# An AdaLN and routed FFN block in fp32: five of the last block's seven products taken to a second level of Strassen's scheme

## The chip, the cores and the metric

The kernel runs on one core of a Trainium2 chip. The metric is device time in microseconds (us): the median of three runs was 262.04 us (261.8 to 263.51). One execution was recorded by the profiler; it took 261.56 us, of which the profile's span covers 259.8 us. All data are float32.

The engines are named as the profile names them: PE (TensorE, matrix products into the PSUM banks), ACT (ScalarE), DVE (VectorE), POOL (GpSimd) and SP, which here only issues transfers.

## The reference, cut to what matters

There are 64 batches of 64 rows, 512 features wide. Two matrix products of 4096 x 512 x 512 bound the work.

```python
# first part: y = relu(((n*v + sum_n v) * relu(q@W3 + b3)) @ W2 + b2)
q_emb = relu(q @ W3 + b3)
y = relu(((n * v + v_sum) * q_emb[:, None, :]) @ W2 + b2)
# second part, on y
base_out   = y @ W_base + b_base
shared_out = (y @ A_s) @ B_s
gates      = softmax(y @ W_router + b_router)          # 6 experts
topk_w, topk_i = top_k(gates, 2)                       # w_per_e: weight of each expert, 0 if not chosen
hw = einsum('bsd,edr->bser', y, A_r) * w_per_e[..., None]
routed_out = einsum('bser,erf->bsf', hw, B_r)
out = x + base_out + shared_out + routed_out
```

## The kernel before

The tokens are cut into four blocks (`NB`) of 1024. Features lie on the 128 partitions, in four chunks of 128; a block's tokens lie along the free axis in two halves of 512 (`TB`). The main loop runs over the blocks k = 0 to 3. Each block has two products: the *first* makes y from the modulated input and `w2_sb`, the *second* makes the output from y and `wb_sb`. Between them a small product (L779, tile `ph`) computes the 112 low-rank activations (16 shared, 6 x 16 routed) and the 6 router logits of every token.

Both large products use the Strassen-Winograd scheme. Features and tokens are halved, and seven products P1 to P7 of half size stand in place of eight. Sums of the weights (`weight_sums`) and sums of the activations (`row_sums`, tile `sy`) are their operands. P1 and P2 make the quarter C11 of the output; with U = P1 + P6, C12 is U + P5 + P3, C21 is U + P7 + P4 and C22 is U + P7 + P5. A seed is an ACT copy from one PSUM bank to another (`seed`, L629), into which TensorE then accumulates the next product. In the first product of blocks 1 to 3 (`first_inner`) each of the seven is again cut into seven matmuls of 128 x 128 x 256 columns, q1 to q7, with two banks for each of the seven rounds (a and b), seeds on ACT, and sums taken out by DVE and ACT (`take_w5`, `take_u`, `take_22`, `take_1`, `take_21`).

The second product (`second`) has one level: each of P1 to P7 is two output chunks of two matmuls of 512 columns (`product`, L168 to L170), written by hand in the order in which it is to run on TensorE. During it DVE runs the gate (`gate`: softmax, ranks of the experts, weights `w`), then multiplies the activations in `ph` by the weights (tile `hw`, L683). TensorE turns `hw` by eight transposes (tile `pt`, L704), ACT copies them out (`hwT`, L706), POOL makes the difference of the two halves (`hwd`, L708), and TensorE adds the routed part to each of the eight output banks by a matmul of `bcat_sb` with `hwT` or `hwd` (L641). The base bias (`bb_sb`) is added by DVE together with x (`with_x`, L637). DVE adds from the bank to the x rows (`leave`, L662), and SP sends them out. x rows are loaded anew for this by `load_rows` into the buffers of the first product's temporaries.

In blocks 0 to 2, DVE and ACT also prepare the next block in the meantime: a list of steps, `behind`, is drawn upon by `fill` and `share`. In the last block that list is empty. There the last output chunk is split in 384 and 128 columns, the second sent by ACT's queue (L650 to L663).

The order of instructions on each engine is the order in which the program issues them; waits between engines are put in by the framework from what each instruction reads and writes. Tiles of a pool wait until a buffer is free: `ps_p` has six PSUM banks, `ps_h` the place of `ph` and `pt`, `xpool` three places of 16 KB a partition.

Of the kernel before, what the change touches and what calls it, by code (L numbers as in the profile page):

```python
# [9 lines left out]
F32 = mybir.dt.float32  # L10
# [22 lines left out]
HC = GR + E  # L33


@with_exitstack
def adaln_ffn(ctx: ExitStack, tc: tile.TileContext, xa, x0, x1, head, w3, w2, wb, a, bcat, br, outT):
# [47 lines left out]
    NH0 = NQ * B + 3 * NC  # L85
    head_sb = const.tile([P, NH0 + NQ * P], F32, tag="head_sb", name="head_sb")
    cond_sb = head_sb[:, : NQ * B].rearrange("p (c b) -> p c b", c=NQ)
    b3_sb, b2_sb, bb_sb = (head_sb[:, NQ * B + n * NC : NQ * B + (n + 1) * NC] for n in range(3))
# [30 lines left out]
    bcat_sb = loaded(bcat, [GR, D], "bcat_sb")  # L119
    load_x(1)  # L120

# [22 lines left out]
    def inner_weight_sums(w, t, name):  # L144

        at = {i: n for n, i in enumerate((5, 6, 7, 4, 1, 2, 3))}
        it = const.tile([P, 4, 7, P], F32, tag=name, name=name)

        def side(o, n):
            b = {1: t[o][:, 0, :P], 2: t[o][:, 1, :P], 3: t[o][:, 1, P:]}  # L150
            return b[n] if n in b else it[:, {5: 0, 6: 1, 7: 2, 4: 3}[n], at[o]]

        low = w.rearrange("p (o k) m -> p o k m", k=KH)
        groups = ((slice(0, 4), lambda c, m: t["sums"][:, :, c, ts(m, P)]),
                  (slice(4, 6), lambda c, m: low[:, :, c, ts(m, P)]),
                  (slice(6, 7), lambda c, m: t[3][:, c, ts(m, P)].unsqueeze(1)))
        steps = []
        for o, b in groups:
            i = [it[:, n, o] for n in range(4)]
            steps += [  # L160
                lambda i=i, b=b: nc.vector.tensor_tensor(i[0], b(0, 1), b(0, 0), ALU.subtract),
                lambda i=i, b=b: nc.vector.tensor_tensor(i[1], b(1, 1), i[0], ALU.subtract),
                lambda i=i, b=b: nc.vector.tensor_tensor(i[2], b(1, 1), b(0, 1), ALU.subtract),
                lambda i=i, b=b: nc.vector.tensor_tensor(i[3], b(1, 0), i[1], ALU.subtract),
            ]
        return side, steps
# [88 lines left out]
    def row_sums(a, name, cols=slice(0, TB)):  # L255

        all_s = mid.tile([P, 4, KH, TB], F32, tag=name, name=name)
        s = [all_s[:, i, :, cols] for i in range(4)]
        a11, a12, a21, a22 = a[:, :KH, 0, cols], a[:, KH:, 0, cols], a[:, :KH, 1, cols], a[:, KH:, 1, cols]

        def steps(c=slice(0, KH)):
            return [
                lambda: nc.vector.tensor_tensor(s[0][:, c], a21[:, c], a22[:, c], ALU.add),
                lambda: nc.vector.tensor_tensor(s[1][:, c], s[0][:, c], a11[:, c], ALU.subtract),
                lambda: nc.vector.tensor_tensor(s[2][:, c], a11[:, c], a21[:, c], ALU.subtract),
                lambda: nc.vector.tensor_tensor(s[3][:, c], a12[:, c], s[1][:, c], ALU.subtract),
            ]

        return {1: a11, 2: a12, 3: s[3], 4: a22, 5: s[0], 6: s[1], 7: s[2], "sums": all_s}, steps
# [28 lines left out]

    def prepare_inner(k):
# [13 lines left out]
        def steps(g, a, engine=nc.vector):  # L313
            return [
                lambda: engine.tensor_tensor(s[g][:, 0], a(0, 1), a(1, 1), ALU.add),
                lambda: engine.tensor_tensor(s[g][:, 1], s[g][:, 0], a(0, 0), ALU.subtract),
                lambda: engine.tensor_tensor(s[g][:, 2], a(0, 0), a(0, 1), ALU.subtract),
                lambda: engine.tensor_tensor(s[g][:, 3], a(1, 0), s[g][:, 1], ALU.subtract),
            ]

# [253 lines left out]
    def gate(k, ph):  # L574
# [10 lines left out]
        nc.scalar.activation(g, lg, AF.Exp)  # L585
        sm = small.tile([P, 2 * NS], F32, tag="sm", name=f"sm_{k}")
# [11 lines left out]
        nc.vector.tensor_tensor(eq, gj, ge, ALU.is_equal)  # L598
        nc.vector.tensor_tensor(gt, gj, ge, ALU.is_gt)
        nc.vector.tensor_tensor(eq, eq, tri.unsqueeze(1).to_broadcast(pair), ALU.mult)  # L600
        nc.vector.tensor_tensor(gt, gt, eq, ALU.add)
        rank = small.tile(shape, F32, tag="rank", name=f"rank_{k}")
# [13 lines left out]
    def second(k, y, ph, res):  # L616
# [17 lines left out]
        def with_x(name, j, f, h):  # L634

            t = row(f, h)
            nc.vector.scalar_tensor_tensor(t, ps[name, j], bb_sb[:, f : f + 1], t, ALU.add, ALU.add)  # L637
            return t
# [9 lines left out]
        def part(p, cols, i, start):  # L648
            for c in range(KH):
                nc.tensor.matmul(  # L650
                    p[:, cols], tb[i][:, c, ts(1, P)], sy[i][:, c, cols], start=start and c == 0, stop=False,
                    skip_group_check=True,
                )

        def last_routed(p, cols, hw):
            nc.tensor.matmul(
                p[:, cols], bcat_sb[:, ts(KH + 1, P)], hw[:GR, cols], start=False, stop=True,
                skip_group_check=True,
            )

        def leave(p, f, h, add, cols=slice(0, TB), queue=nc.sync):
            nc.vector.tensor_tensor(add[:, cols], p[:, cols], add[:, cols], ALU.add)  # L662
            queue.dma_start(outT[k, f, h, :, cols], add[:, cols])  # L663
# [5 lines left out]
        def share():  # L669
# [12 lines left out]
        hw = small.tile([P, 2 * NS, GR], F32, tag="hw", name=f"hw_{k}")  # L682
        nc.vector.tensor_tensor(  # L683
            hw.rearrange("p s (g r) -> p s g r", r=R),
            ph[:, :, :GR].rearrange("p s (g r) -> p s g r", r=R),
            w.unsqueeze(3).to_broadcast([P, 2 * NS, G, R]),
            ALU.mult,
        )
# [12 lines left out]
        pt = ps_h.tile([P, 2 * NS, P], F32, tag="ph", name=f"pt_{k}")  # L701
        hwT = small.tile([P, 2, TB], F32, tag="hwT", name=f"hwT_{k}")
        for s in range(2 * NS):
            nc.tensor.transpose(pt[:GR, s, :], hw[:, s, :], ident)  # L704
        for h in range(2):
            nc.scalar.copy(hwT[:GR, h], pt[:GR, ts(h, NS)].rearrange("p s t -> p (s t)"))  # L706
        hwd = small.tile([P, TB], F32, tag="hwd", name=f"hwd_{k}")
        nc.gpsimd.tensor_tensor(hwd[:GR], hwT[:GR, 0], hwT[:GR, 1], ALU.subtract)  # L708
# [4 lines left out]
        routed("x", 0, 0, hwT[:GR, 0])  # L713
        finish("x", 0, 0, 0)
        routed("z", 0, 0, hwT[:GR, 1])
        finish("z", 0, 0, 1)

        routed("w", 0, KH, hwT[:GR, 1])
        leave(ps["w", 0], KH, 1, u22[0])
        share()  # L720
        if k < NB - 1:
            prod(5, 1, "w")
            routed("w", 1, KH + 1, hwT[:GR, 1])
            leave(ps["w", 1], KH + 1, 1, u22[1])
        else:
            last = [(ps_p.tile([P, TB], F32, tag="pp", name=f"last_{lo}"), slice(lo, hi), queue)
                    for lo, hi, queue in ((0, 3 * P, nc.sync), (3 * P, TB, nc.scalar))]
            for p, cols, queue in last:
                part(p, cols, 5, True)
                last_routed(p, cols, hwT[:, 1])  # L730
                leave(p, KH + 1, 1, u22[1], cols, queue)
        share()
        routed("x", 1, 1, hwT[:GR, 0])
# [3 lines left out]
        routed("z", 1, 1, hwT[:GR, 1])  # L737
# [3 lines left out]
        routed("w", 0, KH, hwd[:GR])  # L741
        leave(ps["w", 0], KH, 0, u12[0])
        share()
        if k < NB - 1:
            prod(3, 1, "w", start=False)
            routed("w", 1, KH + 1, hwd[:GR])
            leave(ps["w", 1], KH + 1, 0, u12[1])
            return
        for p, cols, queue in last:
            part(p, cols, 3, False)  # L750
            last_routed(p, cols, hwd)
            leave(p, KH + 1, 0, u12[1], cols, queue)
# [4 lines left out]
    inner_t, inner_steps = inner_weight_sums(w2_sb, t2, "inner_t")  # L757
    for k in range(NB):
        y = mid.tile([P, NC, 2, TB], F32, tag="y", name=f"y_{k}")
        rest = None  # L760
        if k == 0:
            first_mixed(y)
        else:
            rest = first_inner(k, y)
        res = load_rows(k)
        if k == 0:
            load_x(3)

        ph = ps_h.tile([P, 2 * NS, P], F32, tag="ph", name=f"ph_{k}")
        groups = [(h, s) for h in range(2) for s in range(NS)]
        if not rest:
            groups.sort(key=lambda g: g[1] // KH)
        for n, (h, s) in enumerate(groups):
            if rest and n == 2:
                rest()
            for c in range(NC):
                nc.tensor.matmul(  # L779
                    ph[:, h * NS + s, :HC], y[:, c, h, ts(s, P)], a_sb[:, c, :],  # L780
                    start=(c == 0), stop=(c == NC - 1),
                )
        sys_[k], steps = row_sums(y, "sy")
        for step in steps():
            step()
        fill(4 if k else 9)
        second(k, y, ph, res)
# [50 lines left out]
```

## Time and profile before

| what | us |
|---|---|
| median of three runs | 262.04 (261.8 to 263.51) |
| the profiled execution | 261.56 |
| its span | 259.8 |
| PE busy | 254.8 (98%) |
| DVE busy | 193.9 (75%) |
| ACT busy | 136.5 (53%) |
| POOL busy | 38.7 (15%) |
| last block: router's groups (L779) end, second product begins | 224.69 |
| last matmul ends | 256.56 |
| last DVE add ends | 256.88 |

The times in the profile's rows are microseconds from the span's start, and the mean durations in its groups are nanoseconds. A matmul of float32 appears as two records. "Idle before" is the time that an engine stood still before an instruction, with what released it.

### The profile page before, as it was taken

What the parts mean: (1) busy time and instruction counts of PE and PEld (TensorE: products, weight loads), DVE (VectorE), ACT (ScalarE), POOL (GpSimd) and SP (SyncE); (2) the same over time, 40 slices, a digit from 0 to 9 for tenths busy, and PEclk for the clock granted to TensorE, in tenths of its full rate; (3) what the DMA queues carried; (4) which work ended last, traced back from release to release, by engine and by line L of the source; (5) the groups of instructions that cost most, each with busy time, mean ns of one, the idle gap of its engine ahead of it and who ended that gap; (6) DMA issues with size and microseconds to landing.
All of it is one profiled execution on the core that took longest, in us unless ns stands there. A gap on an engine that the chain in (4) does not pass through costs nothing.

```text
span 259.8 us, 3177 instructions
## 1 busy us (share of the span) xinstructions
PE 254.8 (98%) x1004; PEld 164.5 (63%) x1004; DVE 193.9 (75%) x386; ACT 136.5 (53%) x373; POOL 38.7 (15%) x53
## 2 busy tenths in 40 slices
PE   7999999999999999999999999999999999999995
PEld 3756896454478888444458889544447889745453
DVE  2899898799968967968995894988895475872332
ACT  2399496596048896289017889349404428112000
POOL 1000000020017610002006630002001770000100
PEclk9999999999999999999999999999999999999999
DMA  6997629303320044000521025200332023400233
GB/s 194 360 352 295 261 99 390 156 3 121 121 81 0 11 156 161 0 3 6 196 81 42 0 83 168 76 0 3 121 121 81 0 77 92 159 0 3 76 139 108
DMA packets 14145, 28.54 MB, mean 110 GB/s; under 512 B 1472, under 2 KB 2496, under 8 KB 14128
## 3 DMA queue, kind: packets, MB, share of 16 engines
q1 hardware_dynamic: 13840, 28.21, 30.6%
q8 instruction: 8, 0.13, 0.2%
q10 hardware_dynamic: 288, 0.13, 0.2%
q14 instruction: 9, 0.07, 0.1%
HBM read 19.94 MB, written 8.39 MB: 109 GB/s over the span
## 4 chain that ended last, share of the span: by engine, by line
PE 94%; ACT 2%; DMA 2%; SPq 0%; issue 0%; DVE 0%
PE ia L446 13%; PE ph L779 11%; PE oz L170 11%; PE ox L170 11%; PE ib L446 10%; PE ow L170 9%; PE py L354 5%; PE oy L170 5%; PE ow L641 5%; PE oz L641 3%; PE ox L641 3%; DMA w_sb<-in_w_dram 2%; PE yw L170 1%; PE pt L704 1%; PE last L650 1%; PE yz L170 1%
## 5 line engine op out<-in xcount | busy, mean ns | idle before, releaser
L212 ACT ACTIVATE x<-x,vsum,nq 128x64 f32<-128x64 f32 x192 | 67.5, 431 | 7.0 <-DVE vsum L208 7.0
L779 PE MATMUL ph<-a_sb,y 128*128 128x118 f32 x256 | 30.5, 276 | 0.3 <-ACT y L340 0.3
L779 PEld LDWEIGHTS ph<-a_sb,y 128*128 128x128 f32 x256 | 30.0, 192 | 1.2 <-ACT y L340 0.7
L437 DVE TENSOR_TENSOR u<-ib,u 128x256 f32<-128x256 f32 x42 | 16.4, 419 | 18.5 <-PE ib L446 18.3
L452 ACT COPY ib<-ia 128x256 f32<-128x256 f32 x21 | 7.6, 361 | 42.3 <-PE ia L446 42.3
L170 PE MATMUL ox<-y,wb_sb 128*128 128x512 f32 x64 | 29.5, 593 | 0.0
L708 POOL TENSOR_TENSOR hwd<-hwT 112x512 f32<-112x512 f32 x4 | 5.8, 1452 | 136.1 <-ACT hwT L706 136.1
L170 PEld LDWEIGHTS ox<-y,wb_sb 128*128 128x128 f32 x64 | 11.9, 190 | 13.4 <-issue 13.2
L437 DVE TENSOR_TENSOR u<-ia,u 128x256 f32<-128x256 f32 (+1 forms) x36 | 16.1, 462 | 2.9 <-ACT u L484 1.6
L446 PE MATMUL ib<-inner_s,inner_t 128*128 128x256 f32 x60 | 17.8, 384 | 0.0
L340 ACT ACTIVATE y<-u,head_sb 128x256 f32<-128x256 f32 (+1 forms) x30 | 15.8, 585 | 3.8 <-DVE u L412 3.2
L637 DVE SCALAR_TENSOR_TENSOR xu<-oz,head_sb,xu 128x512 f32<-128x512 f32 x16 | 12.0, 749 | 7.3 <-PE oz L170 4.8
L207 DVE TENSOR_REDUCE vsum<-x 128x8 f32<-128x512 f32 x24 | 16.2, 676 | 0.0
L170 PE MATMUL oz<-sy,tb 128*128 128x512 f32 x32 | 15.2, 599 | 0.0
L170 PE MATMUL oz<-y,tb 128*128 128x512 f32 x32 | 15.1, 593 | 0.0
L170 PE MATMUL oy<-sy,tb 128*128 128x512 f32 x32 | 15.0, 592 | 0.0
L354 PE MATMUL py<-v,w_sb 128*128 128x512 f32 (+1 forms) x40 | 14.4, 510 | 0.7 <-DMA w_sb<-in_w_dram 0.7
L170 PE MATMUL ow<-sy,tb 128*128 128x512 f32 x28 | 13.2, 592 | 0.0
L170 PE MATMUL ow<-sy,wb_sb 128*128 128x512 f32 x28 | 13.2, 592 | 0.0
L455 ACT COPY ib<-ib 128x256 f32<-128x256 f32 x21 | 7.6, 363 | 10.0 <-PE ib L446 10.0
L446 PEld LDWEIGHTS ib<-inner_s,inner_t 128*128 128x128 f32 x60 | 11.2, 190 | 2.2 <-ACT ib L455 0.8
L250 ACT ACTIVATE v<-x,vsum,nq 128x64 f32<-128x64 f32 x32 | 11.0, 427 | 1.7 <-DVE vsum L248 1.7
(173 smaller groups left out, 461.6 us busy)
## 6 DMA issues: line engine op xcount, KB each, us to landing
xu<-in_x_dram SPq DMA_DIRECT2D x16, 512.0 KB, 4.2
out_dram<-xu SPq DMA_DIRECT2D x30, 256.0 KB, 2.0
x<-in_x_dram SPq DMA_DIRECT2D x12, 512.0 KB, 7.5
x<-in_x_dram SPq DMA_DIRECT2D x7, 256.0 KB, 5.7
w_sb<-in_w_dram SPq DMA_DIRECT2D x4, 256.0 KB, 5.5
wb_sb<-in_wb_dram SPq DMA_DIRECT2D x4, 256.0 KB, 4.9
w_sb<-in_w_dram SPq DMA_DIRECT2D x1, 384.0 KB, 4.7
out_dram<-xu SPq DMA_DIRECT2D x2, 192.0 KB, 1.9
```

The costliest lines, as they stand in the source:

```text
L170: nc.tensor.matmul(ps, w[i][:, c, ts(j, P)], s[i][:, c, :], start=start and c == 0, stop=c == KH - 1, skip_group_check=True,)
L207: nc.vector.tensor_reduce(vsum[:, c, bs], xc, AX.XY, ALU.add)
L212: nc.scalar.activation(x, x, AF.Identity, bias=vsum[:, c, b : b + 1], scale=nq[:, c, b : b + 1])
L250: nc.scalar.activation(v[:, c, :, ts(b, NH)], batches_of(c, b, b + 1)[:, :, 0], AF.Identity, bias=vsum[:, c, b : b + 1], scale=nq[:, c, b ...
L340: nc.scalar.activation(y[:, f, h, cols], src, AF.Relu, bias=b2_sb[:, f : f + 1])
L354: nc.tensor.matmul(p[:, :, lo * NH : hi * NH], w2_sb[:, c, ts(f, P)], v[:, c, :, lo * NH : hi * NH], start=(c == 0 and lo == 0), stop=(c = ...
L437: add = lambda o, a, b: nc.vector.tensor_tensor(o, a, b, ALU.add)
L446: nc.tensor.matmul(bank[b, t][:, cols], t_side(o, n), s_side(o, n), start=n == 1, stop=True, skip_group_check=True,)
L452: nc.scalar.copy(bank["b", t][:, lo], bank["a", t][:, lo])
L637: nc.vector.scalar_tensor_tensor(t, ps[name, j], bb_sb[:, f : f + 1], t, ALU.add, ALU.add)
L641: nc.tensor.matmul(ps[name, j], bcat_sb[:, ts(f, P)], hw, start=False, stop=True, skip_group_check=True)
L779: nc.tensor.matmul(ph[:, h * NS + s, :HC], y[:, c, h, ts(s, P)], a_sb[:, c, :], start=(c == 0), stop=(c == NC - 1),)
```

## The change

In the last block the second product no longer runs in `second` but in a new function, `second_inner`. P1, P2, P5, P4 and P3 are cut to a second level there, in this order, as in the first product; P6 and P7 stay on one level. The parts are these:

- P1's first three small matmuls (q1, q5, q6) stand between the router's last groups on TensorE (`two[n]()`).
- The activations' second-level sums are made by POOL for P1, P5, P4 and P3, by DVE for P2. Of the four row sums the last goes to POOL, behind P4's. P5's sums use the places of P2's.
- `gate` takes steps between its own: the small matmuls and takes of P1 and P2 are issued among its DVE instructions.
- The seeds of P6 come from SBUF (`p1`) and those of P7 from P6's banks; the latter stand on ACT ahead of the copies of the turned activations.
- P1 + P2 is added to C11 on POOL, and the routed part of C11 has two banks of its own (`pr`), which DVE adds. For P5, P4 and P3 the routed part is accumulated in the small rounds: q1's and q5's banks take it for the left half of the tokens, and the right half by `n == 22` and by the difference of two weight chunks, `bcat_d`.
- C22 = x22 + U + P7 + P5 is finished by POOL, all but P7's and U's part. Outputs leave in pieces of 256 columns, P3's right half by ACT's queue.
- In all blocks the base bias becomes a 113th row (`GB` = `GR` + 1) of `bcat_sb`, with a row of ones in `hw` (now one constant tile), so `with_x` adds only x.
- The weights' second-level sums (`inner_tb`) are made by POOL in blocks 1 and 2, and `bcat_d` in block 0, each behind the routed difference.

```diff
+    bcat_sb = const.tile([GB, D], F32, tag="bcat_sb", name="bcat_sb")
+    nc.sync.dma_start(bcat_sb[:GR], bcat)
     load_x(1)
+    nc.sync.dma_start(bcat_sb[GR:], bb)
...
-            nc.vector.scalar_tensor_tensor(t, ps[name, j], bb_sb[:, f : f + 1], t, ALU.add, ALU.add)
+            nc.vector.tensor_tensor(t, ps[name, j], t, ALU.add)
...
+        hwT = turn(k)
+        hwd = difference(k, hwT)
+        for step in beside[k]:
+            step()
...
-            for p, cols, queue in last:
-                part(p, cols, 5, True)
-                last_routed(p, cols, hwT[:, 1])
-                leave(p, KH + 1, 1, u22[1], cols, queue)
...
+        order = (1, 2, 5, 4, 3)
+        plus = {1: None, 2: x11, 5: None, 4: x21, 3: x12}
+        out = {1: p1, 2: x11, 5: p5, 4: x21, 3: x12}
+        place = {1: (0, (0, 1, 2, 3)), 2: (1, (0, 1, 2, 3)), 5: (1, (3, 1, 2, 0)), 4: (2, (0, 1, 2, 3)),
+                 3: (3, (0, 1, 2, 3))}
+        run(sums_of(1, of_y(0, 0), nc.gpsimd))
...
+        def row_side():
+            run(sums_of(2, of_y(KH, 0)))
+            got, steps = row_sums(y, "sy")
+            sy.update(got)
+            steps = steps(fourth=nc.gpsimd)
+            run(steps[:3])
+            fourth.extend(steps[3:])
+
+        def late_sums():
+            of_s = lambda o: lambda c, r: sy[o][:, c, ts(r, R2)]
+            run(sums_of(5, of_s(5), nc.gpsimd))
+            run(sums_of(4, of_y(KH, 1), nc.gpsimd))
+            run(fourth)
+            run(sums_of(3, of_s(3), nc.gpsimd))
...
+        routed_of = {5: ("second", KH), 4: ("second", 0), 3: ("less", KH)}
+        def routed(t, n):
...
+            if n == 1:
+                for j, cols in ((1, hi), (0, lo)):
+                    accumulate(bank["a", t][:, cols], w[j], hw[:, lo])
+            elif n == 22:
+                accumulate(bank["b", t][:, hi], w[1], hw[:, hi])
+            else:
+                accumulate(bank["b", t][:, hi], bcat_d[:, f // KH], hw[:, hi])
...
+        def passed_on(t, j, cols):
+            o = order[t]
+            if o == 5:
+                add(x12[:, j, cols], x12[:, j, cols], p5[:, j, cols])
+                add(x22[:, j, cols], x22[:, j, cols], p5[:, j, cols], nc.gpsimd)
+            if o in (5, 4, 3):
+                f, h, t = {5: (KH, 1, x22), 4: (0, 1, x21), 3: (KH, 0, x12)}[o]
+                j = slice(j, j + 1) if isinstance(j, int) else j
+                queue = nc.scalar if o == 3 and cols == hi else nc.sync
+                queue.dma_start(
+                    outT[k, f + j.start : f + j.stop, h, :, cols].rearrange("f p t -> p f t"), t[:, j, cols]
+                )
...
+        def main_part(ph):
+            open_banks(1)
+            q(1, 1)
+            q(5, 1)
+            seed_y(1)
+            def first():
+                q(7, 0)
+                q(3, 0)
+                q(6, 1)
+                seed_z(1)
+                q(2, 0)
+                take(0, bank["a", 0], lo, 0, lo)
+                take_w5(1)
+                take_22(0)
+            gate(k, ph, (first, lambda: add(p1[:, 1, lo], bank["a", 0][:, hi], p1[:, 1, lo])))
+            q(4, 0)
+            take_21(0)
...
+            weigh(k, ph)
+            late_sums()
+            take_1(1)
+            for j in range(KH):
+                seed(j, "y", p1[:, j])
+                product(bank["y", j], 6, j, tb, sy, start=False)
+            q(4, 1)
+            take_21(1)
+            for j in range(KH):
+                seed(j, "z", bank["y", j])
+                add(x12[:, j], bank["y", j], x12[:, j])
+            product(bank["z", 0], 7, 0, tb, sy, start=False)
+            hwT = turn(k)
+            hws["second"] = hwT[:GB, 1]
+            product(bank["z", 1], 7, 1, tb, sy, start=False)
+            for j in range(KH):
+                for x in (x21, x22):
+                    add(x[:, j], bank["z", j], x[:, j])
+            add(x11, x11, p1, nc.gpsimd)
+            hws["less"] = difference(k, hwT)[:GB]
+            for t in (2, 3):
+                open_banks(t)
+                q(1, t)
+                q(5, t)
+                seed_y(t)
+                take_w5(t)
...
+            for j in range(KH):
+                accumulate(pr[:, j], bcat_sb[:, ts(j, P)], hwT[:GB, 0], True)
+            add(x11, pr, x11)
+            leave(0, 0, x11)
+            q(2, 2)
+            q(6, 2)
+            take_u(2)
...
+            q(4, 4)
+            routed(4, 4)
+            take_21(4)
...
+        wide["t"], steps = inner_weight_sums(
+            wb_sb, tb, place[:, : 20 * P].rearrange("p (n o m) -> p n o m", n=4, o=5), (5, 4), nc.gpsimd
+        )
+        beside[1], beside[2] = steps[:4], steps[4:]
```

## The prediction

> **What bounds the kernel now.** I read four views: busy shares, TensorE's waits, the last stage as a stretch by itself, and the chain that ended last. First the page's head, then the waits of TensorE over the whole span:
>
> ```profile
> span 259.8 us, 3177 instructions
> PE 254.8 (98%) x1004; PEld 164.5 (63%) x1004; DVE 193.9 (75%) x386; ACT 136.5 (53%) x373; POOL 38.7 (15%) x53
> ...
> PE idle L181 <- PEq L824: 0.8, 1, 0.8
> PE py L354 <- DMA w_sb<-in_w_dram: 0.7, 1, 0.7
> PE ph L779 <- ACT y L340: 0.3, 2, 0.2
> ```
>
> TensorE waits 1.8 us in all, none of it in the stage that changes. That stage, the last block's second product, starts at 224.69 and its last matmul ends at 256.56 (the columns are stretch, its length, then busy us of each engine):
>
> ```profile
> 224.69:256.57 31.88, 31.86 (x92) 15.63 (x91) 14.37 (x27) 3.51 (x7) 1.26 (x1) 1.00 0.17 61
> ```
>
> TensorE is busy 31.86 of 31.88 us at full clock (1.00); DVE 45%, ACT 11%, POOL 4%. The chain there is TensorE alone, then one DVE add:
>
> ```profile
> 224.69 3.44 PE ox L170 x8
> 228.13 1.72 PE oy L170 x4
> ...
> 238.43 0.87 PE pt L704 x8
> ...
> 242.74 0.86 PE ox L641 x2
> ...
> 256.33 0.24 PE last L656 x2
> 256.56 0.02 issue
> 256.59 0.29 DVE xu L662
> ```
>
> One matmul of 512 columns is two records and 0.86 us (1.72 for four records). So fewer TensorE columns here come straight off the end, until another engine is late. From 256.88 (end of that add) to 259.8 lie 2.92 us of the last transfer.
>
> **What the Trainium skill says.** "SBUF — State Buffer", Who interferes with whom: a VectorE instruction with two SBUF inputs and a GpSimd instruction that reads SBUF exclude one another, and the later one waits for the whole of the earlier; with one input in PSUM it doesn't. The trace agrees: an add of two SBUF operands takes 1.76 us beside a POOL instruction, against 0.69 alone, and it ends 0.55 us after POOL does; adds from PSUM (0.41) keep their time beside POOL.
>
> ```profile
> 180.08 0.68 DVE L265 TENSOR_TENSOR s<-x 128x512 f32<-128x512 f32 x1
> 180.39 1.50 POOL L708 TENSOR_TENSOR hwd<-hwT 112x512 f32<-112x512 f32 x1 [27.06 <-ACT hwT L706]
> 180.68 1.76 DVE L266 TENSOR_TENSOR s<-x,s 128x512 f32<-128x512 f32 x1
> ```
>
> "GPSIMD Engine Reference", 3.1 Elementwise: a two-input add is some twice as slow there as on VectorE. Here too: 0.73 against 0.42 for 256 elements, 1.27 against 0.69 for 512. "DMA: Bandwidth & Descriptors", Issuing engines are not separate DMA queues: transfers issued by SP and by ACT share the same DMA engines. The trace of before has both at the end but doesn't separate them.
>
> ```profile
> L546 POOL TENSOR_TENSOR u<-u,u 128x512 f32<-128x512 f32 x6 | 7.5, 1271 | 3.3 <-issue 3.2
> L315 POOL TENSOR_TENSOR inner_two<-x 128x256 f32<-128x256 f32 x3 | 2.2, 726 | 55.6 <-PE ib L446 55.6
> L437 DVE TENSOR_TENSOR u<-ia,u 128x512 f32<-128x512 f32 x6 | 4.1, 688 | 0.5 <-PE ia L446 0.2
> ```
>
> **The change on TensorE.** Before: 28 matmuls of 512 (24.1), 8 routed ones (6.9) and the transposes (0.87): 31.9, as measured. After: five of seven products become 7 matmuls of 256 columns each. One of 256 is 0.43 us: the first product's stage, which already works on two levels, ran 48 of them in 21.0 us (196.11 to 217.12), 0.37 more than 48 x 0.43. So 35 x 0.43 = 15.05, two products as before 8 x 0.86 = 6.88, transposes 0.87, routed 2 x 0.86 + 12 x 0.43 = 6.88. Sum 29.68: **2.2 us less**. The 113th row that brings the bias into the routed matmuls adds no columns. Three of the 35 stand between the router's groups of L779, so those now end at T0 = 224.69 + 1.29 = 225.98, and TensorE ends at T0 + 28.4 = 254.4 instead of 256.57, if nothing waits.
>
> **Does anything wait?** I laid the instructions out in the order of each engine, with the durations of the rows, and 0.2 us from a matmul's end to its reader (L437 starts 0.21 after the matmul before it). Times are after T0.
> - *The first ten small matmuls* after T0 end at 4.30. The seed of P6 is an ACT copy of 512 (0.57) behind the copy of P1's last quarter (0.37), whose matmul ends at 3.01: 3.2 + 0.37 + 0.57 = 4.2. Just in time; I allow 0.1.
> - *Gate.* DVE now has four sums of 256 (4 x 0.35) between L437's last add (219.8) and the row sums; with three of 1.22 they end at 224.95, before T0. The fourth row sum went to POOL. Gate and weighing took 5.25 us (225.72 to 230.97); with five adds from PSUM put between (0.35 each) and 0.5 for one collision with POOL, the weighed activations are ready at about T0 + 7.7. The transposes come at 9.9: 2.2 us of slack. The x rows for C11 land at 219.49 + 4.6 = 224.1, first used at T0 + 1.
> - *POOL* is the new long server. Its sums for the third product reuse the second's places, so they wait for that product's q3, ending at 3.87. From 4.1 on: 12 sums of 256 (0.715 apart: 77.13 to 79.99 for four) = 8.6, the row sum of 1024 and C11's of 1024. Size 1024 is in no row; the slope from 256 to 512 gives 2.36, twice the 512 row 2.54, and I take 2.36. POOL is done with C11 at 4.1 + 8.6 + 4.7 = 17.4, with the difference (1.26) at 18.7. TensorE asks for POOL's sums at 12.9 and later, each ready 4 us sooner or more.
> - *The wait added on DVE.* The add of the routed part to C11 (1024 from PSUM, 1.23 by the slope) waits for POOL until 17.6; behind it in DVE's order are an add of 0.4 and the take of P5's lower right quarter, and TensorE's q4 of that product overwrites that quarter at 20.66. The quarter itself is complete at 19.36, so DVE is done at 20.0: 0.7 us of slack, and about 0.8 for POOL. The later quarters have 1.1 or more, less up to 1 where DVE adds two SBUF operands beside POOL's sums for C22.
> - *Banks* of the two-level rounds come free 2 us or more ahead.
>
> So on the likeliest course TensorE stays the bound: -2.2 + 0.1.
>
> **The tail.** The last add has 256 columns (0.42, was 0.29): +0.13. Its transfer is 128 KB behind one of 256 KB issued 0.6 us earlier; it was 64 KB (1.7 to landing) behind 192 KB (1.9), and 256 KB takes 2.0. By size +0.1; for the two in flight together nothing to +0.5, I take 0.15. Sum **+0.4**.
>
> **Other blocks.** One POOL difference in block 0, four in block 1, eight in block 2: 0.7, 2.9 and some 4.7 us. They stand behind the routed difference, so it isn't later. The next POOL work is at 200.37, some 13 us on. DVE's two-SBUF adds may wait for them, at worst 4.7 us in block 2; TensorE reads the last of those sums (done 197.0) at 201.9 by its order of 0.43 each. Cost nothing; if the cover were gone, under 1 us. The bias leaves DVE's adds (0.75 to 0.69), off the path. SP gets one small load behind block 1's rows, POOL one memset, both in the first stage: nothing.
>
> **Sum.** 259.8 - 2.2 + 0.1 + 0.4 = 258.1 span, 261.56 - 1.7 = 259.9 for the profiled execution. That one lay 0.5 below the median of 262.04, so against the median: **260.3**.
>
> **Rivals.** (a) *Small exchanges cost TensorE.* The two-level stage of before had 0.37 us of loss in 48; here two chains (seed of P6, quarters of P5) have under 1 us of slack, and a late copy of 0.3 to 0.5 each, with a tail at its upper bound, gives 261.2. For it: ACT and DVE handshakes were modelled, not seen; against: the first product's stage has the same handshakes. (b) *POOL becomes the bound*, the one that ends slower. Place: the C11 add on DVE that waits for POOL, with P5's quarter behind it. It decides from 0.8 us of POOL lateness; beyond that each us goes to TensorE. If POOL's 14 instructions each lose 0.2 to VectorE's lock and the two of 1024 take 2.8, it is 3.7 late: 2.9 lost, 263.2. For it: the difference took 1.50 beside VectorE, 1.26 alone. Against: VectorE's work in that stretch is from PSUM. (c) *TensorE was never worth so much*: the outgoing transfers set the end. Eleven output transfers (2 MB) now leave in the last 10 us of the stage, where before the same bytes left over 13. If they queue for 1.5 us, 261.8; against it, DMA was busy 17% in this stage.
>
> **Chances.** Forecast 0.66, (a) 0.18, (b) 0.09, (c) 0.07. Range 259.6 (tail at no cost, and the run-to-run spread of 0.3) to 261.8, which takes in (a) and leaves (b). A change under 1% (2.6 us) can't be told from none: faster by over 1% would need more than TensorE's whole 2.2, unless the transfers ended sooner too: 0.06; within 1%: 0.89; slower by over 1%, (b) at its worst: 0.05.
>
> **What would show it.** Right: TensorE's last stage some 2.2 us shorter with no wait row over 0.2, the last add at about 255.0 of the span, C11's routed add on DVE released by POOL and near T0 + 17.6. Wrong: TensorE waiting on DVE or ACT in the two-level rounds, POOL's 1024 rows over 2.8, or over 3.5 us from the last add to the end.

## The result and the profile after

The changed kernel took 259.51 us (median of four runs, 259.28 to 259.86), the kernel before 261.92 in the same comparison: a ratio of 0.9899, 95% interval 0.9855 to 0.9943. Two repeats with more runs of the kernel before gave 0.9927 (0.9910 to 0.9944) and 0.9925 (0.9910 to 0.9940), so 1.9 to 2.0 us less. The forecast was 1.7 us less and 260.3, with a range from 259.6 to 261.8. The direction was right; the time lies 0.09 below the range. The first ratio is itself just over the 1% that the forecast gave as the likely limit; the two repeats, with narrower intervals, put the gain at 0.7 to 0.8%.

The profiled execution took 259.86 us, the highest of its four runs, and its span is 258.1; the forecast for it was 259.9 and 258.1. First the page's head, then the waits of PE over the whole span, then the last stage as a stretch. It starts at 224.86, where the router's groups would have ended without the three small matmuls between them (226.15 less 1.29), so that it can be set beside 224.69 to 256.57 of before:

```profile
span 258.1 us, 3326 instructions
PE 252.6 (98%) x1034; PEld 170.6 (66%) x1034; DVE 199.6 (77%) x404; ACT 142.7 (55%) x391; POOL 68.8 (27%) x88
...
PE py L361 <- DMA w_sb<-in_w_dram: 0.8, 1, 0.8
PE idle L187 <- PEq L1115: 0.8, 1, 0.8
PE ph L1066 <- ACT y L347: 0.3, 2, 0.2
```

```profile
224.86:254.74 29.88, 29.84 (x126) 22.15 (x125) 19.58 (x42) 9.06 (x23) 18.04 (x18) 1.00 0.18 61
```

PE has the same three waits as before and none in the last stage. It is busy 29.84 of 29.88 us there; before it was 31.86 of 31.88. POOL has gone from 1.26 to 18.04 us, DVE from 14.4 to 19.6. The chain that ended last is still PE, then one add:

```profile
226.15 0.87 PE ja L820 x4
...
230.48 3.49 PE oy L176 x8
233.97 0.43 PE jb L820 x2
234.40 1.72 PE oz L176 x4
236.12 0.87 PE pt L597 x8
236.99 1.72 PE oz L176 x4
...
253.83 0.88 PE jb L820 x4
254.72 0.03 issue
254.74 0.42 DVE xu L776
```

From the last matmul's end to the end of the span it is 3.38 us (254.72 to 258.1); before it was 3.24 (256.56 to 259.8). So 1.84 us went off the time to the last matmul's end and 0.14 came back behind it. The last stage itself is 2.0 shorter, but it began 0.17 later in this execution (224.86 against 224.69).

The place of the forecast's narrowest margin, in order of time on POOL and DVE (start, duration, instruction):

```profile
238.52 0.73 POOL L307 TENSOR_TENSOR inner_y<-sy 128x256 f32<-128x256 f32 x1
...
241.38 2.36 POOL L776 TENSOR_TENSOR xu<-xu,parts 128x1024 f32<-128x1024 f32 x1
243.69 1.28 POOL L604 TENSOR_TENSOR hwd<-hwT 113x512 f32<-113x512 f32 x1
```

```profile
243.77 1.23 DVE L776 TENSOR_TENSOR xu<-pr,xu 128x1024 f32<-128x1024 f32 x1 [2.49 <-POOL xu L776]
244.91 0.41 DVE L776 TENSOR_TENSOR xu<-jb,xu 128x256 f32<-128x256 f32 x1
245.72 0.42 DVE L776 TENSOR_TENSOR parts<-jb,parts 128x256 f32<-128x256 f32 x1 [0.39 <-ACT jb L848]
```

DVE waits 2.5 us for POOL's sum for C11 and starts its own add at 243.77, which is T0 + 17.6 with T0 = 226.15, as forecast. It is free at 245.3 and then stands 0.39 us. The row names a copy on ACT, but the matmul that completes P5's quarter ends at 245.62 as well, and in e5 below the same take begins (245.88) before that copy does (245.99), so it is the matmul that DVE waits for. The quarter is taken by 246.14, and PE's q4, which overwrites it, starts at 246.75:

```profile
245.02 0.60 PE L820 MATMUL jb<-hwT,bcat_sb 113*128 113x256 f32 x2
...
246.75 0.59 PE L820 MATMUL jb<-sy,inner_tb 128*128 128x256 f32 x2
```

The long wait on DVE costs nothing, and 0.39 and 0.61 us are left before it would.

### The profile page after: what moved, and what is told of

It is laid out like the page before. It is cut to its first block, busy times and chain, and to the rows that moved or that the text cites. A ratio compares the mean times of both kernels' runs of the same rounds, so it can differ in the third digit from the quotient of the medians.

```text
span 258.1 us, 3326 instructions
## 1 busy us (share of the span) xinstructions
PE 252.6 (98%) x1034; PEld 170.6 (66%) x1034; DVE 199.6 (77%) x404; ACT 142.7 (55%) x391; POOL 68.8 (27%) x88
## 4 chain that ended last, share of the span: by engine, by line
PE 94%; ACT 2%; DMA 2%; SPq 0%; issue 0%; DVE 0%
PE ia L453 13%; PE ph L1066 11%; PE ib L453 10%; PE oz L176 9%; PE ox L176 8%; PE ow L176 8%; PE py L361 5%; PE oy L176 5%; PE ja L820 4%; PE ow L683 4%; PE jb L820 4%; PE ox L683 2%; PE oz L683 2%; DMA w_sb<-in_w_dram 2%; PE yw L176 1%; PE pt L597 1%
## 5 line engine op out<-in xcount | busy, mean ns | idle before, releaser
L604 POOL TENSOR_TENSOR hwd<-hwT 113x512 f32<-113x512 f32 x4 | 5.6, 1393 | 109.4 <-ACT hwT L599 109.4
L176 PE MATMUL ox<-y,wb_sb 128*128 128x512 f32 x48 | 22.1, 593 | 0.0
L176 PEld LDWEIGHTS ox<-y,wb_sb 128*128 128x128 f32 x48 | 8.9, 190 | 10.0 <-issue 9.6
L361 PE MATMUL py<-v,w_sb 128*128 128x512 f32 (+1 forms) x40 | 14.4, 510 | 0.8 <-DMA w_sb<-in_w_dram 0.8
L307 POOL TENSOR_TENSOR inner_two<-x 128x256 f32<-128x256 f32 x3 | 2.2, 727 | 45.0 <-PE ib L453 45.0
L361 PEld LDWEIGHTS py<-v,w_sb 128*128 128x128 f32 x40 | 7.4, 190 | 6.5 <-issue 4.5
L176 PE MATMUL oz<-y,tb 128*128 128x512 f32 x24 | 11.3, 592 | 0.0
L176 PE MATMUL ow<-sy,tb 128*128 128x512 f32 x24 | 11.3, 592 | 0.0
```

The source lines that it names most:

```text
L176: nc.tensor.matmul(ps, w[i][:, c, ts(j, P)], s[i][:, c, :], start=start and c == 0, stop=c == KH - 1, skip_group_check=True,)
L361: nc.tensor.matmul(p[:, :, lo * NH : hi * NH], w2_sb[:, c, ts(f, P)], v[:, c, :, lo * NH : hi * NH], start=(c == 0 and lo == 0), stop=(c = ...
```

## The experiments

All but the third are edits of the changed kernel. Several chips served; each comparison has runs of the kernel before on its own chip, so differences between chips are taken by the ratios. Theory T: PE's columns are the whole of the gain, and the rest has slack of the size forecast.

**The difference measured more closely** (e1 and e11, no edit).

> The changed kernel as it is, to measure the difference more closely. Theory T (TensorE's columns are the whole of it: 31.87 us of last stage became 29.86 in the traces, and the way from the last matmul to the end grew by 0.14): 1.9 us faster than before, between 1.6 and 2.2. Rival S (something besides the last stage was saved too, since the medians so far differ by 2.4): 2.3 or more.

> The changed kernel once more. The traces' sum is 2.0 less on TensorE and 0.15 more after it, 1.85 in all; the first repeat gave a ratio of 0.9927 (1.9 us), the medians at the result 2.4. T: the ratio lies at 0.993, 1.6 to 2.1 us. If it lies at 0.991 or less (2.35 us or more), 0.5 us of the gain is not in the last stage as traced.

Measured: 259.53 against 261.65 (51 runs of the kernel before), ratio 0.9927, 1.91 us; then 260.01 against 261.76, 0.9925, 1.96 us. T's sum of the traces is 1.85. Each interval alone reaches up to 2.35 us, the edge of S; the two together, and the traces, speak for T. From the start of the router's groups to the end of the last matmul the traces give:

| run | groups start | last matmul ends | between |
|---|---|---|---|
| before | 217.12 | 256.57 | 39.45 |
| only the other edits (e2) | 217.34 | 256.79 | 39.45 |
| changed kernel | 217.29 | 254.72 | 37.43 |
| again (e1) | 216.76 | 254.19 | 37.43 |
| again (e11) | 217.68 | 255.11 | 37.43 |

This stretch repeats to 0.01 us and is 2.02 shorter. What differs from run to run lies ahead of it: the same program reaches the groups at times 0.9 us apart. The 2.4 us of the first comparison is put down to that scatter in four runs.

**Only the edits outside the last block's second product** (e2).

```diff
-        two = second_inner(k, y, res) if k == NB - 1 else None
+        two = None
...
+        if k < NB - 1:
+            prod(5, 1, "w")
...
+        for p, cols, queue in last:
+            part(p, cols, 3, False)
+            last_routed(p, cols, hwd)
+            leave(p, KH + 1, 0, u12[1], cols, queue)
```

> All edits outside the last block's second product are kept (bias as a 113th row, VectorE's adds without it, POOL's weight sums and the difference of the low-rank weights, which are computed and not used), and that product is as before, its last chunk split in 384 and 128. T: 0.0 against the kernel before, within 0.2. S: these edits bring 0.4 or more of the gain.

Measured: 261.46 against 261.65, ratio 0.9993 (0.9985 to 1.0000): 0.2 us faster, between 0 and 0.4. The bias in the routed matmuls and POOL's weight sums cost nothing that can be told, and hardly bring anything; the last stretch is as long as before (39.45). The trace of block 2 shows POOL's extra work delaying itself and DVE, with nothing behind it:

```profile
185.85 0.95 POOL L168 TENSOR_TENSOR inner_tb<-wb_sb,inner_tb 128x128 f32<-128x128 f32 x1
186.77 0.90 POOL L169 TENSOR_TENSOR inner_tb<-wb_sb 128x128 f32<-128x128 f32 x1
```

```profile
186.52 0.83 DVE L270 TENSOR_TENSOR s<-s,x 128x512 f32<-128x512 f32 x1
187.27 0.94 DVE L271 TENSOR_TENSOR s<-x 128x512 f32<-128x512 f32 x1
...
196.00 1.22 DVE L310 TENSOR_TENSOR inner_s<-s,inner_s 128x1024 f32<-128x1024 f32 x1
```

POOL's sums of 128 elements take 0.90 to 0.95 here, beside DVE's adds of two SBUF operands, and one a little earlier, beside an add from PSUM, takes 0.45. DVE's last sum for the next block still ends at 197.2 (197.0 before). POOL's eight sums run from 182.02 to about 188.5: 6.5 us, where 4.7 were forecast.

**The tail by itself** (e3, an edit of the kernel before).

```diff
-                    for lo, hi, queue in ((0, 3 * P, nc.sync), (3 * P, TB, nc.scalar))]
+                    for lo, hi, queue in ((0, 2 * P, nc.sync), (2 * P, TB, nc.scalar))]
```

> The kernel before with its last chunk split in 256 and 256 columns instead of 384 and 128: the size of last piece that the changed kernel has. The prediction's term for the tail was +0.4 (0.13 for the add, 0.1 for the size, 0.15 for two transfers in flight). If that holds: +0.25 to +0.4 on the way from the last matmul's end to the end of the span. If the traces' +0.14 holds, the add alone pays: +0.1 to +0.2.

Measured: ratio 1.0007 (0.9999 to 1.0015). The chain that ended last:

```profile
256.05 0.45 PE last L656 x2
256.50 0.02 issue
256.52 0.42 DVE xu L662
```

The span is 259.8, so it is 3.30 us from the last matmul to the end, against 3.24. The add is 0.13 longer, and from the add's end to the end of the span it is 2.86 with 128 KB, against 2.92 with 64 KB. The span is given to 0.1 us, so these two don't differ. The last 128 KB add nothing against the last 64 KB of the kernel before, and in the changed kernel, where 256 KB go out ahead of them, it is 2.94: the prediction's 0.25 for size and crowding wasn't there. The kernel before had crowding of its own, 192 KB issued 0.4 us ahead of its last 64.

**P7's second seed behind the turned activations** (e4).

```diff
             for j in range(KH):
-                seed(j, "z", bank["y", j])
                 add(x12[:, j], bank["y", j], x12[:, j])
...
             hws["second"] = hwT[:GB, 1]
+            seed(1, "z", bank["y", 1])
```

> In the changed kernel, the seed of P7's second chunk is put behind the two copies of the turned activations on ACT. T: the copies end at about 238.1 of the span, the seed takes 0.57, so TensorE starts that product near 238.75 instead of 236.99: a wait of 1.75, and all of it at the end, 1.5 to 2.0 slower than the changed kernel. Rival (TensorE's later waits have room and take it up): under 0.5 slower.

Measured: 261.88, ratio 1.0015 (1.0003 to 1.0027): slower than the kernel before; the whole gain is gone.

```profile
PE oz L176 <- ACT oz L910: 1.7, 1, 1.7
```

```profile
236.90 1.07 ACT L599 COPY hwT<-pt 113x512 f32<-113x512 f32 x2 [4.17 <-PE pt L597]
237.86 0.61 ACT L910 COPY oz<-oy 128x512 f32<-128x512 f32 x1
238.52 1.98 PE L176 MATMUL oz<-sy,tb 128*128 128x512 f32 x4 [1.65 <-ACT oz L910]
```

The first view is PE's waits, the second is in order of time. The order on ACT alone costs PE 1.65 us of wait, and 1.9 of delay: q4 of P2 starts at 233.68 and the last matmul ends at 256.51, against 233.80 and 254.72 without the edit. That is within the 1.5 to 2.0 expected. By the medians it is 2.35, which is 0.4 more than the trace; that part stays open.

**More work on POOL ahead of C11's sum** (e5, e6), and **the waiting add moved behind the take of P5's quarter** (e7).

```diff
+            for _ in range(1):                     # e6, e7: range(2), 512 columns
+                nc.gpsimd.tensor_tensor(spare, y[:, 0, 0, :256], y[:, 1, 0, :256], ALU.add)
             add(x11, x11, p1, nc.gpsimd)
...
-            add(x11, pr, x11)                      # e7 only
-            leave(0, 0, x11)
...
             take_22(2)
+            add(x11, pr, x11)                      # e7 only
+            leave(0, 0, x11)
```

> In the changed kernel POOL makes one more sum of 256 elements, not used, ahead of C11's (0.73 and the gap, 0.8 us). T with the forecast's slack of 0.8 us: VectorE's add to C11 starts 0.8 later, the take of P5's quarter ends at about 246.55 of the span, TensorE's q4 asks at 246.75: 0.0 to 0.2 slower than the changed kernel. Rival B (POOL is already the bound there): 0.8 slower.

> As the last, with two sums of 512 (2.6 us with gaps). T: 2.6 less the slack of 0.8 to 1.1, on TensorE's wait for VectorE at q4 of P5: 1.5 to 1.8 slower than the changed kernel. If POOL's lateness were taken up by later slack: under 0.5.

> The two sums of 512 stay, but VectorE's add to C11 stands behind the take of P5's quarter in VectorE's order. T (the cost is the queue behind one waiting instruction, not POOL's speed or the port): the wait at q4 of P5 is gone; VectorE then has 1.2 us more ahead of P4's quarter, which has 1.1 of room: 0 to 0.9 slower than the changed kernel, at least 0.8 less than with the add in its old place. Rival (the port, or POOL's later sums): as slow as with the old place, 1.5 or more.

Measured on one chip: 259.50, 261.35 and 260.17 (ratios 0.9909, 0.9982 and 0.9963). The changed kernel had no run on this chip. Against e5, e6 is 1.85 slower and e7 0.67; by the ratios, against 0.9926 for the changed kernel on other chips, it is 1.5 and 1.0. The traces are sharper. From the start of the router's groups to the last matmul's end it is 37.43 us in e5, as without the edit, 39.06 in e6 and 38.09 in e7. So C11's sum 0.7 us later is free, 2.6 later costs 1.6, and 2.6 with the add moved costs 0.7. PE's waits in e6 and then in e7:

```profile
PE jb L821 <- DVE parts L777: 1.4, 1, 1.4
```

```profile
PE jb L821 <- DVE xu L777: 0.4, 1, 0.4
```

The slack at this place is 0.9 us, and what costs most is the queue behind one waiting instruction on DVE. It isn't POOL's speed as such: with the same work on POOL, some three fifths of the cost go when DVE's order changes. The rest is a stop at q4 of P4. Ahead of it on DVE stand the moved add and two adds of SBUF operands that run beside POOL's sums for C22; which of these costs it was not separated. This is the prediction's rival (b) made real: at 2.6 us of lateness most of the gain is gone.

**A smaller last piece** (e8), and **with a PSUM bank of its own** (e9).

```diff
+            own = ps_p.tile([P, TB], F32, tag="pp", name="own")          # e9 only
+            nc.scalar.copy(own[:, :P], bank["b", 4][:, R2 + P :])        # e9 only
...
-            q(4, 4)
-            routed(4, 4)
-            take_21(4)
+            b4, less = bank["b", 4], hws["less"]
+            for p, at, n, queue in ((b4, R2, 0, nc.sync), (own, 0, 1, nc.scalar)):   # e8: both in b4
+                cols = slice(R2 + n * P, R2 + (n + 1) * P)
+                accumulate(p[:, at : at + P], t_side(3, 4), s_side(3, 4)[:, ts(n, P)])
+                accumulate(p[:, at : at + P], bcat_d[:, 1], less[:, cols])
+                add(x12[:, 0, cols], p[:, at : at + P], x12[:, 0, cols])
+                queue.dma_start(outT[k, KH, 0, :, cols], x12[:, 0, cols])
```

> The changed kernel with the last quarter of C12 in two pieces of 128 columns, the first by SP's queue, the second by ACT's. T (the way from the last matmul to the end is a fixed 2.9 us after the last add, plus that add): the add goes from 0.42 to 0.29, and the end comes 0.1 to 0.15 sooner, TensorE's time being the same. If small matmuls of 128 columns cost more than half of one of 256 (0.43): up to 0.2 slower.

> As the last (the last quarter of C12 in two pieces of 128), but the second piece has a PSUM bank of its own, into which ACT copies its part of U + P7 ahead of time. T: the wait of 0.54 that TensorE had for VectorE's read of the first piece came from the shared bank and is gone; TensorE ends as in the changed kernel, the last add takes 0.29 instead of 0.42, so 0.1 to 0.15 from the last matmul to the end is saved, hardly to be told from none in the medians. Rival (the two pieces cost TensorE themselves): the last stage is longer by 0.3 or more.

Measured: ratios 0.9926 (0.9904 to 0.9949) and 0.9920 (0.9893 to 0.9947), no change against the changed kernel's 0.9927 and 0.9925. An effect of 0.1 us could not show in these medians, so the traces have to tell. In e8 TensorE's time was expected to stay the same, but it doesn't: PE waits 0.54 for DVE's read of the first piece, though it writes other columns of that bank:

```profile
254.44 0.28 DVE L776 TENSOR_TENSOR xu<-jb,xu 128x128 f32<-128x128 f32 x1
254.78 0.49 PE L820 MATMUL jb<-sy,inner_tb 128*128 128x128 f32 x2 [0.54 <-DVE xu L776]
```

In e9 that wait is gone, as expected. But DVE still adds the 512 columns of the piece before (254.18 to 254.87) when the small pieces come, and they queue behind it:

```profile
254.18 0.69 DVE L776 TENSOR_TENSOR xu<-ja,xu 128x512 f32<-128x512 f32 x1 [0.69 <-PE ja L820]
254.65 0.39 PE L820 MATMUL own<-hwd,bcat_d 113*128 113x128 f32 x2
254.79 0.28 DVE L776 TENSOR_TENSOR xu<-jb,xu 128x128 f32<-128x128 f32 x1
255.07 0.29 DVE L776 TENSOR_TENSOR xu<-own,xu 128x128 f32<-128x128 f32 x1
```

From the router's groups to the end of the last add it is 37.77 us (217.59 to 255.36), against 37.87 in the changed kernel (217.29 to 255.16), the 0.1 expected. Then the two transfers are issued at 255.38 and 255.40, and from the last add to the end it is 3.14 us instead of 2.94. In e8, where PE's stop keeps the two transfers 0.8 apart, it is 2.48 (255.82 to 258.3). So my theory of a fixed 2.9 fell: by these two traces, transfers issued close together cost some tenths, and what the smaller add saves is given back there. Neither version can be told from the changed kernel.

**P1's small matmuls behind the router's groups** (e10).

```diff
-            if two and n in two:
-                two[n]()
...
+            two[6]()
+            two[7]()
             two["all"](ph)
```

> In the changed kernel P1's first three small matmuls stand behind all of the router's groups instead of between them. Columns are the same. T: q6 of P1 waits for its seed, 0.2 from the matmul's end and 0.36 for the copy, against 0.43 of other work: a wait of about 0.2 and nothing else, so 0.1 to 0.3 slower. Rival (the place matters for the gate and for the seeds behind it): 0.6 or more slower.

Measured: 260.81, ratio 0.9956 (0.9942 to 0.9971): 0.8 us slower than the changed kernel by the ratios, against 0.1 to 0.3 expected. The chain:

```profile
224.96 0.89 PE ja L820 x4
225.85 0.02 issue
225.87 0.36 ACT jb L845
226.24 0.14 issue
226.37 0.67 PE jb L820 x2
227.04 0.86 PE ja L820 x4
227.91 0.08 issue
227.99 0.67 PE jb L820 x2
```

The rival's size (0.6 or more) came, not mine. PE stops twice where I had one stop of 0.2. The first stop has a wait row of 0.54; the second has none, only 0.08 of issue. The two records after each stop take 0.67 where they take 0.43 in a stream. From the groups' start (217.39) to the last matmul's end (255.91) it is 38.52 us, against 37.43 without the edit, 1.1 more. So placing them between the groups hides both seeds and is worth 0.8 to 1.1 us, about half of the gain.

## Why the prediction was right or wrong, point by point

- **What bounds the kernel: right.** PE has no wait in the last stage before or after, and the stretch is PE's busy time in both.
- **TensorE's columns, 2.2 less: right, 0.2 too much.** The stage went from 31.87 to 29.86 (2.0). A small matmul in a stream takes 0.433 rather than 0.43 (eight records 1.73), which over 47 of them is some 0.13; P6's eight records took 3.49 where 3.44 were counted. Together that is the 0.2.
- **The first ten small matmuls, 0.1 allowed: no wait came.** P6's seeds end in time; the products start at 230.48, T0 + 4.33, against 4.30.
- **Gate: right.** One add of two SBUF operands took 0.87 beside POOL instead of 0.46, which is the collision that was priced at 0.5. The weighed activations were ready at 233.65, T0 + 7.5, against 7.7 forecast; the transposes started at T0 + 10.0.
- **POOL: right.** Size 1024 took 2.36 and 2.37, the slope's value; the C11 sum ended at 243.74, T0 + 17.6, against 17.4. That a DVE instruction with two SBUF inputs and a POOL instruction that reads SBUF hold each other up, as the Trainium skill has it in "SBUF — State Buffer", Who interferes with whom, shows in this stage in both directions: 0.87 for DVE's add, and 0.82 and 0.83 for POOL's first sums against 0.73.
- **The wait added on DVE and its slack of 0.8: right**, 0.9 measured. e5 and e6 show it from both sides, and e7 shows most of its mechanism.
- **The tail, +0.4: wrong in size.** It measured 0.14 in the trace of the result. The add's 0.13 is all of it; the 0.1 for the size and the 0.15 for two transfers in flight weren't there. e3 shows the size without the other edits. Crowding shows in e8 and e9 (2.48 and 3.14 after the last add). The kernel before, with 2.92, probably paid it too, so that the term counted as new what was there already; that is argued, not shown.
- **Other blocks at no cost: right** (e2, 0.9993).
- **The sum, and the step that failed.** For one profiled execution the terms that missed nearly cancel: PE gave 0.1 less than 2.2 - 0.1, the tail cost 0.25 less than forecast, so 1.85 in place of 1.7. That the span came out at exactly the 258.1 forecast is luck: this execution began its last stage 0.17 later than the one before. What failed is the step "That one lay 0.5 below the median of 262.04, so against the median: 260.3". It took the place of one execution among three as a property of the kernel. Of the changed kernel the profiled execution lay 0.35 above its median (259.86 and 259.51), not 0.5 below, and these two offsets together are the miss of 0.8. The median of 262.04 was high: over 51 later runs on one chip it was 261.65, near the profiled 261.56. By this steadier figure 0.4 of the miss is the offset, 0.15 the tail's and PE's terms, and the remaining 0.25 is within what single comparisons of this kernel scatter (259.51, 259.53 and 260.01 for the same program).
- **The range: too narrow at its low end.** It was built on the same high median, with 0.3 for the spread from run to run. Three runs of the kernel before had spread over 1.7 us already, and six of the changed kernel lay between 259.22 and 260.48 (e1). That a change under 1% can't be told from none was too strict as well: both repeats tell 0.7 to 0.8% from none.
- **Rivals.** (a) did not come: no exchange stopped PE. That it could have is shown by e10, and there each stop cost more than I had priced. (b) did not come, and e6 shows it near the price forecast: 1.5 to 1.8 expected, 1.6 by the trace, 1.5 or 1.85 by the times. (c) did not come: the time from the last add to the end of the span was 2.94, before 2.92, with eleven transfers in the last ten microseconds.

## What to carry to other kernels

Where one engine is busy without a gap, price a change by that engine's own row durations and then list, for each wait that the change adds, what stands behind the waiting instruction and how much slack it has. Here the first gave TensorE's saving to 0.1 us, and the second found the slack of 0.8 to 0.9 behind one waiting add. To overrun that slack by 1.7 us, or to exchange two copies on an engine that is idle most of the stage, cost most or all of the gain. The same pricing fell short where TensorE really stopped (0.1 to 0.3 expected in e10, 0.8 to 1.1 measured).

Forecast the profiled execution or, better, the length of the stage, which repeated to 0.01 us here while the medians of four to six runs moved by 0.5. Don't carry the offset between one execution and a median of three runs over into the forecast.

## What the runs showed that I had not expected

A stop of TensorE cost more than its wait row. In e4 the wait row was 1.65 and the delay 1.9, in e6 1.36 and about 1.63, in e7 0.39 and 0.66, in e8 0.54 and 0.8, at the first stop of e10 0.54 and 0.77: 0.23 to 0.28 more each time. The stop of e6:

```profile
246.09 0.59 PE L821 MATMUL ja<-inner_y,inner_tb 128*128 128x256 f32 x2
248.06 0.70 PE L821 MATMUL jb<-sy,inner_tb 128*128 128x256 f32 x2 [1.36 <-DVE parts L777]
248.59 0.60 PE L821 MATMUL jb<-hwT,bcat_d 113*128 113x256 f32 x2
```

The row counts from the modelled end of the matmul before (246.68). In a stream the next one starts 0.43 after the start, at 246.52, so 0.16 of the delay isn't in the row, and the first matmul after the stop is about 0.1 longer (0.70 against 0.59). That the difference is the lost overlap of two matmuls is argued, not shown.

In this program waits go by the whole tile, here one PSUM bank, and not by column: in e8 PE waited for DVE's read of other columns, and a bank of its own took the wait away (e9). Whether the tile or the bank decides can't be told, since each tile here is one bank. In the changed kernel ACT stands 1.66 us behind an add of DVE that reads the same half bank as ACT's copy and writes none of it, probably for the same reason, at no cost:

```profile
245.36 0.36 ACT L848 COPY jb<-jb 128x256 f32<-128x256 f32 x1 [1.66 <-DVE xu L776]
```
